# The last row frequency's transform back, moved into the next group's products

## The chip, the cores and the metric

The kernel runs on one core of a Trainium2 chip. The metric is device time in microseconds (us) of one execution; the time of a kernel is the median of its runs. Beside the times there is one profiled execution, with a record of every instruction on every engine (TensorE, VectorE, ScalarE, GpSimd, SyncE), of the DMA packets and of the clock that TensorE was granted.

## The reference

The program computes two layers on x of shape (16, 16, 256, 256). The change touches only the first, a Laplace neural operator with poles and residues, in this part of it:

```python
x = x + _L0_conv_ref(_gn(x), ...)          # layer 0
...
alpha = jnp.fft.fft2(x, axes=(-2, -1))
A  = 1.0 / (omega1[:, None, None, None] - weights_pole1[None])
Bm = 1.0 / (omega2[:, None, None, None] - weights_pole2[None])
S = jnp.einsum('ikpq,oikp,xikq->oxik', weights_residue, A, Bm)
output_residue1 = jnp.einsum('biox,oxik->bkox', alpha, S)
...
x1 = jnp.fft.ifft2(output_residue1, s=(Ny, Nx), axes=(-2, -1)).real
```

For every row frequency o and column frequency x a 16 by 16 matrix S mixes the channels of the spectrum; then the result is transformed back. The mix and the transform back along the columns (x) are the stage of the change; the transform along the rows is the next stage. Everything is in float32.

## The kernel before

The program is a string of stages. `layer0_forward` makes the spectrum of the normalised input and writes it to HBM as `al`; `layer0_mix` reads `al`, mixes the channels, transforms back along x and writes `hd`; `layer0_back` reads `hd`, transforms back along y, adds the input and normalises for layer 1; `layer1` is the rest. The change is in `layer0_mix`, which runs from about 1480 to 3050 us.

**Groups.** Real input makes the spectrum symmetric, so 128 row frequencies and one half are enough. `layer0_mix` goes over NF = 33 groups of four row frequencies; the last group has one (`range(4 if more else 1)`). For each group there are six kinds of work.

- `poles` (L609): six VectorE products spread a group's table of poles `av` to `lt`, the weights for the residues. There is one buffer for `lt` and two for `av`; `load_poles` (L599) loads the table of the group after next on SyncE's queue.
- `residues` (L623): TensorE makes S for the next group, two k at a time (eight calls, k0 = 0 to 14); each fills two PSUM tiles of the pool `psg`, copied to `s` by ScalarE for even k (L633) and VectorE for odd k (L631). There is one buffer for `s`.
- `expand` (L593, L595): the spectrum of four images (q of four) is spread to the block form `alb`, which all 16 images share; each q takes four operations, one or two on ScalarE and the others on VectorE. When it is done, `load_spectrum` (L582) loads the next one on SyncE's queue.
- `mix` (L642): the products proper. For each of 256 column frequencies i, a 128x32 weight tile `s[:, i]` is multiplied with `alb[:, i]` (128x64). Four at a time go to the four quadrants of 32 output partitions. There are eight blocks (`x0` = 0, 8, ..., 56) of 32 products each; each block fills one of four `psg` tiles and ScalarE copies it to `y` (L649). A float32 product is two matmul instructions, each with its weight load, so a mix is 512 matmuls and 512 loads, 64 of each in a block.
- `turn` (L658): for one row frequency f, eight TensorE transposes bring `y` into the layout for the transform; VectorE (L664) and ScalarE (L662) copy four of them each to `yt` (two buffers).
- `columns` (L675): the transform back of one row frequency f along x. 16 products (32 matmuls, 32 loads), eight for the even columns (`e` = 0) and eight for the odd ones (`e` = 1), go to two PSUM tiles `ph` (pool `psh`, two buffers). Then, for each tile, ScalarE copies the odd half (L684), VectorE makes sum and difference (L687, L688), and GpSimd issues the write to `hd` (L692), 256 KB.

**The order.** The whole stage is under `tc.manual_schedule` for TensorE, ScalarE, VectorE and GpSimd: each engine runs its instructions in the order of the program text, and only SyncE's loads are placed otherwise. For group g the order is: `mix` of g; `poles` and `residues` k0 = 0 for g + 1; then for each f: `turn`, two more calls of `residues` (one at f = 0), `expand` of q = f for g + 1, the next loads, `columns` of f. So `columns` of f = 3 stands between the last `residues` and `expand` for g + 1 and the `mix` of g + 1. Every product of a mix reads all 16 images of `alb`, and so needs all four expansions.

**Lines of the change.** `mix` gets a third argument; `columns` becomes a generator with a stop between `e` = 0 and `e` = 1; the loop over groups calls them in another order.

Of the kernel before, what the change touches and what calls it, by code (L numbers as in the profile page):

```python
# [547 lines left out]
def layer0_mix(ctx, tc, d, al, hd, tabs):  # L548
# [28 lines left out]
    def load_spectrum(g, q):  # L577

        t = gp.tile([P, 4, 2, P], F32, tag="alc", name="alc", bufs=4)
        src = al[g].rearrange("v (j h c) b x -> h (v j) c (b x)", h=2, c=8)  # L580
        for h in range(2):
            nc.sync.dma_start(  # L582
                out=t[64 * h : 64 * h + 64].rearrange("p b e x -> p (b e x)"),
                in_=src[h, :, :, 4 * q * N : 4 * q * N + 4 * N],
            )
        return t

    def expand(t, q):

        dst = alb.rearrange("p (x e) j b -> p b e x j", e=2)[:, 4 * q : 4 * q + 4]  # L590
        for j in range(4):
            if j <= q % 2:
                nc.scalar.activation(dst[..., j], t, AF.Copy, scale=m4[:, j : j + 1])  # L593
            else:
                nc.vector.tensor_scalar(dst[..., j], t, m4[:, j : j + 1], None, ALU.mult)  # L595

    def load_poles(g):
        av = ap.tile([P, 32, 4, 3], F32, tag="av", name="av")
        nc.sync.dma_start(out=av.rearrange("p k f l -> p (k f l)"), in_=avd[g])  # L599
        return av  # L600

    def poles(av):


        lt = lp.tile([P, 2, C, 3, 4, 8], F32, tag="lt", name="lt")
        shape = [P, C, 4, 8]
        for h in range(2):
            for plane in range(3):
                nc.vector.tensor_tensor(  # L609
                    lt[:, h, :, plane],  # L610
                    av[:, 16 * h : 16 * h + 16, :, plane].unsqueeze(3).to_broadcast(shape),
                    m8.unsqueeze(1).unsqueeze(2).to_broadcast(shape),
                    ALU.mult,
                )
        return lt

    def residues(lt, s, k0):

        for k in range(k0, k0 + 2):
            ps = psg.tile([P, 2, N], F32, tag="pg", name="ps")  # L620
            for v in range(2):
                for h in range(2):
                    nc.tensor.matmul(  # L623
                        ps[64 * h : 64 * h + 64, v],
                        lhsT=lt[:, h, k, 1 - v : 3 - v].rearrange("p l f c -> p (l f c)"),
                        rhs=tt[:, h, k],
                        start=True,
                        stop=True,
                    )
            if k % 2:  # L630
                nc.vector.tensor_copy(s[:, :, :, k], ps.rearrange("p v x -> p x v"))  # L631
            else:
                nc.scalar.copy(s[:, :, :, k], ps.rearrange("p v x -> p x v"))  # L633

    def mix(s, y):

        for x0 in range(0, 64, 8):
            ps = psg.tile([P, 8, 64], F32, tag="pg", name="pg")
            for x in range(8):
                for q in range(4):  # L640
                    i = 4 * (x0 + x) + q
                    nc.tensor.matmul(  # L642
                        ps[32 * q : 32 * q + 32, x],
                        lhsT=s[:, i].rearrange("p v k -> p (v k)"),
                        rhs=alb[:, i].rearrange("p j b -> p (j b)"),
                        start=True,
                        stop=True,
                    )
            nc.scalar.copy(y[:, :, x0 : x0 + 8], ps.rearrange("p x j -> p j x"))  # L649

    def turn(y, f):

        yt = hp.tile([P, 8, 8, C], F32, tag="yt", name="yt", bufs=2)
        for t0 in range(0, 8, 4):
            pt = pst.tile([P, 4, P], F32, tag="pt", name="pt")
            for t in range(4):
                j = 16 * f + 2 * (t0 + t)
                nc.tensor.transpose(pt[:, t], y[:, j : j + 2].rearrange("p q x -> p (q x)"), ident)  # L658
            dst = yt[:, :, t0 : t0 + 4].rearrange("p c t k -> p t c k")
            src = pt.rearrange("p t (c k) -> p t c k", k=C)  # L660
            if t0:
                nc.scalar.copy(dst, src)  # L662
            else:
                nc.vector.tensor_copy(dst, src)  # L664
        return yt

    def columns(g, f, yt):

        ph = [psh.tile([P, 2, N], F32, tag="ph", name="ph") for q in range(2)]
        for e in range(2):  # L670
            for n, (c, v) in enumerate(((0, 0), (0, 1), (1, 0), (1, 1))):
                i = 2 * (2 * c + e) + v
                for q in range(2):
                    lanes = slice(64 * q, 64 * q + 64)
                    nc.tensor.matmul(  # L675
                        ph[q][:, e],
                        lhsT=yt[lanes, i].rearrange("p t k -> p (t k)"),
                        rhs=ix[lanes, i],
                        start=n == 0,
                        stop=n == 3,  # L680
                    )
        for q in range(2):
            odd = hp.tile([P, 2, P], F32, tag="odd", name="odd", bufs=2)
            nc.scalar.copy(odd, ph[q][:, 1].rearrange("p (v x) -> p v x", v=2))  # L684
            o = hp.tile([P, 2, 2, P], F32, tag="h", name="h", bufs=5)
            even = ph[q][:, 0].rearrange("p (v x) -> p v x", v=2)
            nc.vector.tensor_tensor(o[:, :, 0], even, odd, ALU.add)  # L687
            nc.vector.tensor_tensor(o[:, :, 1], even, odd, ALU.subtract)  # L688
            o = o.rearrange("p v h x -> p v (h x)")
            fy = 4 * g + f  # L690
            if fy % P:
                nc.gpsimd.dma_start(  # L692
                    out=hd[fy, q:nb:2].rearrange("b k v x -> b (k v x)"),
                    in_=o.rearrange("p v x -> p (v x)"),
                )
            else:
                part = fy // P
                nc.gpsimd.dma_start(out=hd[0, q:nb:2, :, part], in_=o[:, 0])

    E = mybir.EngineType  # L700
    with tc.manual_schedule(engines={E.PE, E.Activation, E.DVE, E.Pool}):
        spectrum = [load_spectrum(0, q) for q in range(4)]
        lt = poles(load_poles(0))
        av = load_poles(1)
        s = gp.tile([P, N, 2, C], F32, tag="s", name="s")
        for k0 in range(0, C, 2):
            residues(lt, s, k0)
        for q in range(4):
            expand(spectrum[q], q)
            spectrum[q] = load_spectrum(1, q)  # L710
        for g in range(NF):
            more = g + 1 < NF
            y = gp.tile([P, 64, 64], F32, tag="y", name="y")
            mix(s, y)
            if more:
                lt = poles(av)
                s = gp.tile([P, N, 2, C], F32, tag="s", name="s")
                residues(lt, s, 0)
            for f in range(4 if more else 1):
                yt = turn(y, f)  # L720
                if more:
                    for k0 in range(2 if f == 0 else 4 * f, 4 * f + 4, 2):
                        residues(lt, s, k0)
                    expand(spectrum[f], f)
                    if g + 2 < NF:
                        if f == 0:
                            av = load_poles(g + 2)
                        spectrum[f] = load_spectrum(g + 2, f)
                columns(g, f, yt)


def exponential(nc, pool, y):
# [629 lines left out]
@with_exitstack  # L1362
def forward(ctx, tc, d):
    nb = d["x"].shape[0]
    dram = ctx.enter_context(tc.tile_pool(name="dram", bufs=1, space=DRAM))
    keep = ctx.enter_context(tc.tile_pool(name="keep", bufs=1))
    al = dram.tile([NF, 2, 64, nb, N], F32, name="al")
    bd = dram.tile([nb, P, P], F32, name="bd")
    hd = dram.tile([P, nb, C, 2, N], F32, name="hd")
    tabs = (  # L1370
        dram.tile([P, 2, C, N], F32, name="td"),
        dram.tile([NF, P, 384], F32, name="avd"),
        dram.tile([P, 2, C, N], F32, name="ed"),
    )
    zn = dram.tile([nb, C, N + 2, N + 2], F32, name="zn")
    cf = dram.tile([4, N + 2, 4, C, N], F32, name="cf")
    mr = keep.tile([P, nb, G, 2], F32, name="mr")
    layer0_forward(tc, d, al, bd, tabs)
    layer0_mix(tc, d, al, hd, tabs)
    layer0_back(tc, d, hd, bd, zn, mr, tabs[2])  # L1380
    layer1(tc, d, zn, cf, mr, nb)
# [25 lines left out]
```

## Time and profile before

| | us |
|---|---|
| time, median of 3 runs (7692.57 to 7713.86) | 7697.9 |
| the profiled execution's own time | 7702.15 |
| its span, first to last instruction | 7700.4 |
| TensorE busy with matmuls, of the span | 7126.0 |
| stretch 1480 to 3045 us (the mix stage): TensorE busy | 1379.6 of 1565 |
| same stretch: VectorE busy | 1007.9 |
| same stretch: ScalarE busy | 920.9 |
| same stretch: GpSimd busy | 153.2 |

The mean granted clock of TensorE was 0.965 over the span and 0.96 in the stretch of the mix. One group takes some 48 us of this stretch: about 14.7 us of mix and 33.6 us of all the rest.

How to read the lines that follow. A group line has the source line, the engine, the operation, the tiles (written <- read), the shape and the count; then busy time in all and the mean in ns of one; then the idle time of the engine just before these instructions and what ended most of it. "issue" is idle time in which the engine waited for no semaphore that the profile shows. A line of the timeline has the start and the busy time in us, then the same names, and in brackets the idle time before. PE is TensorE's matmuls, PEld its weight loads, DVE is VectorE, ACT ScalarE, POOL GpSimd, SP SyncE. Matmuls overlap, so that the mean of one is longer than the step from one to the next.

### The profile page before, as it was taken

To read this page: it belongs to the slowest core of one execution; us is meant where nothing else is said; L and a number is where in the kernel's file an instruction comes from. 1 tells how busy PE (TensorE), PEld (TensorE's weight loads), DVE (VectorE), ACT (ScalarE), POOL (GpSimd) and SP (SyncE) were. 2 spreads that over 40 slices of the span, in tenths; PEclk is the share of its full clock that TensorE was granted. 3 is DMA by queue.
4 is the path that set the end of the run, shared out by engine and by line. 5 is a ranking of instruction groups with operands and counts; after the bars stand their busy time and mean duration, and the time that the engine had idled before them with its cause. 6 is when DMAs were issued, how large, how long until landed. Compare 5 with 4: busy or idle time off the path is not lost. (4 is left out here: it accounts for less than half of the span.)

```text
span 7700.4 us, 147483 instructions
## 1 busy us (share of the span) xinstructions
PE 7126.0 (93%) x58728; PEld 4107.7 (53%) x58728; DVE 4921.2 (64%) x9184; ACT 3678.6 (48%) x5387; POOL 2804.5 (36%) x3616
## 2 busy tenths in 40 slices
PE   7889999688888988999978999999999999999997
PEld 5778888566666766777733333333333333333332
DVE  8999865366666665666656666666666666666662
ACT  2223333355555554111146656666566655656662
POOL 2334444200000000111135545555554555555552
PEclk9999999899999999999989999999999999999998
DMA  3444444333333333877757788898888898888896
GB/s 99 112 116 121 120 115 108 111 94 94 94 94 94 92 90 121 261 246 245 246 153 216 217 245 248 260 263 251 249 241 251 249 263 256 248 243 251 246 267 205
DMA packets 936290, 1442.20 MB, mean 187 GB/s; under 512 B 91866, under 2 KB 807958, under 8 KB 903606
## 3 DMA queue, kind: packets, MB, share of 16 engines
q1 hardware_dynamic: 792374, 958.51, 44.6%
q0 software_dynamic: 143232, 474.25, 19.4%
q8 instruction: 469, 7.68, 0.4%
q14 instruction: 215, 1.76, 0.1%
HBM read 875.87 MB, written 556.47 MB: 186 GB/s over the span
## 5 line engine op out<-in xcount | busy, mean ns | idle before, releaser
L995 ACT ACTIVATE wide<-c,b 32x512 f32<-32x512 f32 x2176 | 1479.5, 680 | 372.0 <-PE c L946 319.7
L1023 DVE TENSOR_TENSOR t<-pd,r 64x512 f32<-64x512 f32 x1088 | 744.4, 684 | 1321.8 <-PE pd L1015 1298.9
L1026 DVE TENSOR_TENSOR top<-pd,t 32x512 f32<-32x512 f32 x2176 | 1504.3, 691 | 54.8 <-DMA cf<-top 2.3
L1089 PE MATMUL c2ps<-rows,c 128*32 128x512 f32 x12288 | 1393.4, 600 | 20.6 <-ACT e L1098 14.7
L946 PE MATMUL c<-z,w 102*128 102x512 f32 x2048 | 1053.6, 646 | 140.1 <-ACT wide L995 116.3
L1007 POOL COPY wide<-wide 32x1031 f32<-32x1031 f32 (+1 forms) x576 | 570.1, 990 | 1390.1 <-ACT wide L995 1362.7
L1015 PE MATMUL pd<-wide,dw 128*128 128x512 f32 x2048 | 1012.7, 617 | 6.0 <-ACT r L983 3.2
L1089 PEld LDWEIGHTS c2ps<-rows,c 128*32 128x32 f32 x12288 | 388.7, 109 | 992.3 <-issue 885.1
L946 PEld LDWEIGHTS c<-z,w 102*128 102x128 f32 x2048 | 399.2, 197 | 703.8 <-issue 515.3
L1015 PEld LDWEIGHTS pd<-wide,dw 128*128 128x128 f32 x2048 | 376.7, 194 | 626.5 <-issue 458.2
L692 POOL DMA_DIRECT2D hd<-h x254 | 151.9, 598 | 1373.2 <-DVE h L688 1353.2
L631 DVE COPY s<-ps 128x512 f32<-128x512 f32 x264 | 271.4, 1028 | 508.5 <-PE ps L623 487.2
L1008 POOL COPY wide<-wide 32x1031 f32<-32x1031 f32 (+1 forms) x576 | 573.4, 996 | 35.9
L1098 ACT ACTIVATE e<-c2ps,b 128x512 f32<-128x512 f32 x256 | 176.0, 687 | 855.3 <-PE c2ps L1089 852.7
L313 PE MATMUL px<-wxn,u 128*64 128x256 f32 x4224 | 558.7, 385 | 2.1 <-ACT o L320 1.8
L813 PE MATMUL py<-h,iy 128*128 128x256 f32 x2048 | 541.5, 383 | 5.2 <-issue 5.2
L623 PE MATMUL ps<-tt,lt 128*64 128x256 f32 x4224 | 496.1, 385 | 37.9 <-DVE lt L609 37.3
L642 PE MATMUL pg<-alb,s 128*32 128x64 f32 x16896 | 310.6, 240 | 196.3 <-issue 185.2
L675 PE MATMUL ph<-ix,yt 64*128 64x256 f32 x4128 | 480.4, 382 | 0.7 <-ACT yt L662 0.7
L313 PEld LDWEIGHTS px<-wxn,u 128*64 128x64 f32 x4224 | 401.1, 136 | 127.4 <-ACT o L320 5.3
L813 PEld LDWEIGHTS py<-h,iy 128*128 128x128 f32 x2048 | 385.2, 191 | 108.4 <-issue 50.0
L675 PEld LDWEIGHTS ph<-ix,yt 64*128 64x128 f32 x4128 | 389.0, 187 | 89.9 <-issue 49.2
(202 smaller groups left out, 10343.7 us busy)
## 6 DMA issues: line engine op xcount, KB each, us to landing
rows<-cf SPq DMA_DIRECT2D x128, 2176.0 KB
z<-zn SPq DMA_DIRECT2D x768, 256.0 KB
cf<-top POOLq DMA_DIRECT2D x512, 240.0 KB, 7.3
cf<-bot POOLq DMA_DIRECT2D x96, 840.0 KB, 10.4
alc<-al SPq DMA_DIRECT2D x264, 256.0 KB
zn<-zb SPq DMA_DIRECT2D x128, 516.0 KB
o<-zn SPq DMA_DIRECT2D x64, 1032.0 KB
z<-in_x SPq DMA_DIRECT2D x64, 1024.0 KB
```

The source lines that it names most:

```text
L313: nc.tensor.matmul(ps[64 * k : 64 * k + 64, :, h], lhsT=u[:, h, part, g0 + j + k].rearrange("p f c -> p (f c)"), rhs=wxn[:, h, part], star ...
L623: nc.tensor.matmul(ps[64 * h : 64 * h + 64, v], lhsT=lt[:, h, k, 1 - v : 3 - v].rearrange("p l f c -> p (l f c)"), rhs=tt[:, h, k], start= ...
L675: nc.tensor.matmul(ph[q][:, e], lhsT=yt[lanes, i].rearrange("p t k -> p (t k)"), rhs=ix[lanes, i], start=n == 0, stop=n == 3,)
L813: nc.tensor.matmul(py[:, yh], lhsT=iy[:, v, ys], rhs=h[:, k, v], start=v == 0, stop=False)
L946: nc.tensor.matmul(ps[:, q], lhsT=w, rhs=cols[:, 1 - q], start=True, stop=True)
L995: nc.scalar.activation(self.feat[64 - 32 * q : 96 - 32 * q, f, self.groups[g], :H], ps[32 * f : 32 * f + 32, q], AF.Mish, bias=b1[0][32 * ...
L1007: nc.gpsimd.tensor_copy(flat[0:32, f, 1:m], flat[64:96, f, 0 : m - 1])
L1008: nc.gpsimd.tensor_copy(flat[96:128, f, 0 : m - 1], flat[32:64, f, 1:m])
L1015: nc.tensor.matmul(ps, lhsT=dwt if self.tail else dw, rhs=self.feat[:, f, cs, :H], start=True, stop=True,)
L1023: nc.vector.tensor_tensor(t[64:128], ps[:64], self.r[:, cs], ALU.mult)
L1026: nc.vector.tensor_tensor(self.top[32 * f : 32 * f + 32, cs, q], ps[lanes], t[lanes], ALU.add)
L1089: nc.tensor.matmul(ps[32 * j : 32 * j + 32], lhsT=c2[:, blk, dx, :], rhs=t[:, 4 * j + blk : 4 * j + blk + 4, x : x + H], start=(blk, dx) = ...
```

## The change

The transform back of the last row frequency of a group (f = 3) is no longer run at the end of the group. The generator `columns(g, 3, yt)` is made there, but nothing of it is issued until the next group's mix, which runs its first half (`e` = 0, 16 matmuls) ahead of block `x0` = 24 and the rest (`e` = 1, the odd copies, the sums and the two writes) ahead of block `x0` = 48. For f = 0, 1, 2, and for the one frequency of the last group, the generator is run out at once, so that the order there is as before. This happens in 32 of the 33 mixes; the first has an empty generator. Besides, `poles` of the next group is issued ahead of the mix and not behind it.

```diff
-    def mix(s, y):
+    def mix(s, y, between):
         for x0 in range(0, 64, 8):
+            if x0 in (24, 48):
+                next(between, None)
             ps = psg.tile([P, 8, 64], F32, tag="pg", name="pg")
...
         ph = [psh.tile([P, 2, N], F32, tag="ph", name="ph") for q in range(2)]
         for e in range(2):
+            if e:
+                yield
             for n, (c, v) in enumerate(((0, 0), (0, 1), (1, 0), (1, 1))):
...
+        between = iter(())
         for g in range(NF):
             more = g + 1 < NF
             y = gp.tile([P, 64, 64], F32, tag="y", name="y")
-            mix(s, y)
             if more:
                 lt = poles(av)
+            mix(s, y, between)
+            if more:
                 s = gp.tile([P, N, 2, C], F32, tag="s", name="s")
                 residues(lt, s, 0)
             for f in range(4 if more else 1):
...
-                columns(g, f, yt)
+                between = columns(g, f, yt)
+                if f < 3:
+                    for _ in between:
+                        pass
```

No instruction is added or taken away; only the order changes.

## The prediction

> **What bounds the kernel now.** I read the page first (busy rows, costliest groups), then the stretch 1480 to 3045 us in which the mix runs (its waits and DMA), then the timeline of one turn from group to group, and last the clock in slices of 3.4 us around single waits. The chain that ended last lies in later stages, but the whole program is a string of stages that wait for each other, so a microsecond that the mix gives up or takes is one of the total. In the mix TensorE is the bound, and the only large idle time is in the products on the quadrants:
>
> ```profile
> L642 PE MATMUL pg<-alb,s 128*32 128x64 f32 x16896 | 310.6, 240 | 196.3 <-issue 185.2
> L675 PE MATMUL ph<-ix,yt 64*128 64x256 f32 x4128 | 480.4, 382 | 0.7 <-ACT yt L662 0.7
> ```
>
> Line 642 stood idle for 196 us, almost all of it for "issue", that is for no semaphore at all. The matmuls of the transform back (line 675) wait for nothing. The waits of the stretch name what stands ahead of line 642's first matmul in each group:
>
> ```profile
> PE pg L642 <- issue: 172.4, 90, 4.8
> PE pg L642 <- ACT alb L593: 9.4, 32, 0.3
> ```
>
> 32 times, 0.3 us each, the mix waits for ScalarE to finish the expansion of the spectrum. The timeline of one turn shows why it is so little, and what the issue waits look like:
>
> ```profile
> 2003.67 1.90 PE L623 MATMUL ps<-tt,lt 128*64 128x256 f32 x16
> ...
> 2005.49 3.72 PE L675 MATMUL ph<-ix,yt 64*128 64x256 f32 x32
> 2005.57 3.89 ACT L593 ACTIVATE alb<-alc,m 128x1024 f32<-128x1024 f32 x2
> ...
> 2006.49 2.57 DVE L595 TENSOR_SCALAR alb<-alc,m 128x1024 f32<-128x1024 f32 x2
> ...
> 2009.51 3.44 PE L642 MATMUL pg<-alb,s 128*32 128x64 f32 x232 [0.29 <-ACT alb L593]
> ...
> 2010.76 1.26 POOL L692 DMA_DIRECT2D hd<-h  x2 [6.66 <-DVE h L688]
> 2011.04 3.69 DVE L609 TENSOR_TENSOR lt<-av,m 128x512 f32<-128x512 f32 x6
> ...
> 2015.41 1.99 PE L642 MATMUL pg<-alb,s 128*32 128x64 f32 x128 [2.46 <-issue]
> ...
> 2019.16 1.99 PE L642 MATMUL pg<-alb,s 128*32 128x64 f32 x128 [1.75 <-issue]
> ...
> 2022.90 0.54 PE L642 MATMUL pg<-alb,s 128*32 128x64 f32 x24 [1.75 <-issue]
> ```
>
> Two things are to be seen. First, the 3.72 us of line 675 (the last row frequency, f = 3) lie exactly beside the 3.89 us of line 593: they cover the expansion. Second, the mix restarts every 128 matmuls, 3.75 and 3.74 us apart (2015.41, 2019.16, 2022.90). 128 matmuls with 128 weight loads are 256 instructions, and the stretch has a DMA queue for just that (packets, MB, share of the engines); the second row is the writes of hd (count, KB each, us to landing):
>
> ```profile
> q8 instruction: 204, 3.34, 0.9%
> ...
> hd<-h POOLq DMA_DIRECT2D x254, 256.0 KB, 6.2
> ```
>
> 3.34 MB in 204 packets are 16.4 KB each; the mix is limited by the arrival of its own program, one page of 256 instructions per 3.74 us, against 1.9 us of work in it. Over the 32 mixes that the change touches (groups 1 to 32) single starts in the trace give: mix 14.7 us long on average, first page step 4.1 us, second 4.6, third 3.7.
>
> **The change, part by part.** Per group, 32 groups.
>
> (1) The transform of f = 3 leaves its place ahead of the mix. That frees 3.66 us of TensorE, but the mix can't start sooner: every product reads all 16 images of alb, and ScalarE's order ahead of the last expansion is untouched. TensorE now stands idle from the last residue matmul to 2009.51, by the starts in the trace 3.95 us where it was 0.29. Gain 0. The cover for the expansion is gone.
>
> (2) The same 64 instructions (32 matmuls, 32 loads) now stand in the mix, half of them after 3 of the 8 blocks, half after 6. If the pages set the pace, what they add is their share of a page: 64/256 x 3.74 = +0.94 us, and the other 2.7 us of work lie in time that was idle. Bounds: +0.44 (32 more pairs at 13.7 ns when no more page falls into the mix) and +3.66 (nothing hidden). I take 0.94: a half is 1.86 us, and with 112 pairs at 13.7 ns beside it a page holds 3.4 us of work, still under 3.74.
>
> (3) The writes of f = 3 to hd (two of 256 KB, 6.2 us to land) move from the front of the mix to its end. Now they land some 4 to 7 us into the mix, where the second page is asked for; that step takes 4.6 us where the third takes 3.7. Without them -0.85 us. Bounds: 0 (the spectrum loads of SP, which stay, are what holds the page up) and -1.2 (the first step falls to 3.74 as well). At the new place, after the sixth block and the VectorE sums, they meet code of 58 ns per instruction, where a page has 15 us to come.
>
> (4) The clock. After one long issue wait (2207.83 to 2212.33) it is halved, after one of 2.46 us it isn't:
>
> ```profile
> 2208.50:2212.00 3.50, 0.00 (x0) 0.00 (x0) 1.22 (x3) 0.00 (x0) 0.00 (x0) 0.99 0.77 237
> 2212.00:2215.40 3.40, 3.07 (x116) 3.07 (x120) 0.00 (x0) 0.62 (x2) 0.00 (x0) 0.50 0.03 11
> ...
> 2010.90:2014.30 3.40, 2.06 (x148) 1.89 (x136) 3.40 (x7) 1.54 (x3) 1.05 (x2) 1.00 0.65 171
> 2014.30:2017.70 3.40, 1.99 (x128) 1.83 (x128) 0.43 (x1) 1.17 (x2) 0.00 (x0) 1.00 0.63 204
> ```
>
> The columns: the stretch, its length, busy time (instructions) of TensorE's matmuls and loads, VectorE, ScalarE and GpSimd, then clock, DMA share and GB/s. 116 pairs at half clock take 3.07 us, 26.5 ns each against 13.7. In this trace every 3.4 us slice of the stage that had under 1.25 us of full-rate work was followed by one at 0.50. The new wait of 3.95 us always leaves such a slice, so nearly every mix now starts at half rate. Hidden is what falls behind a page; not hidden is the part ahead of the first page boundary, on average 64 pairs: 64 x (26.5 - 13.7) = 0.8 us, less what of the halved slice is spent in the wait itself. I take +0.7; bounds 0 and +1.7 (half of a slice).
>
> The Trainium skill ("TensorE: Matmul & The Clock Gate", Part 1) states that an idle window of about 3.4 us throttles the array to half, and that the window runs freely; the slices above agree. By the page alone the term would be up to 1.7 us, the sum +60 us. The skill's "Runtime: NRT & Kernel Launch", section "Instruction fetch mechanics", states that crossing a page of instructions is mostly hidden; by it the mix would have no idle time to fill and the change would cost (1)'s whole cover, +117 us. The restarts above contradict it.
>
> (5) TensorE changes its tile shape three times more per group. First columns matmul after the last residue: 0.31 us start to start, where pairs of the same kind follow in 0.22; so 0.1 each. Mostly behind the pages: +0.1, bounds 0 and +0.45.
>
> (6) At nothing: the poles (six of 684 ns on VectorE) run some 2 us earlier; their reader starts at the mix's end, 8.6 us after the old finish, so they had cover and keep it. SP's pole load waits for them and goes out 2 us earlier, 192 KB into a time with little traffic. Behind it SP has only the next group's spectrum. The two odd copies (377 ns) now stand ahead of the last two y copies on ScalarE; the transposes start 1.2 us after the last y copy today, and ScalarE idles for most of the mix. If that cover failed, 0.65 us. The four sums (0.41 us) are done before the first residue copy needs VectorE. POOL idles up to 24.6 us for its two issues. PSUM ph, yt and h are wanted again only after the next group's first transposes.
>
> Sum: 0 + 0.94 - 0.85 + 0.7 + 0.1 = +0.89 us per group, x 32 = **+28 us**. The profiled execution took 7702.15 us (span 7700.4), 4 us over the median; I add the sum to the median 7697.9: **7726 us**. A measurement of this kernel tells about 0.3%, 23 us, from no change.
>
> **The rivals.**
>
> A. As summed, chance 0.52, own range 7685 to 7755: the terms' signs differ, and 0.15 us per group decides whether it passes 0.3%.
>
> B. The halves aren't hidden (0.22). Place: the half-rate clock holds through the first half, which then takes 3.7 us instead of 1.86, and the page behind it has come long before; and the page steps shrink by half of what I take when the writes move. Price: (2) rises by 1.86 to 2.8, (3) is -0.4, (4) and (5) stay: 3.2 us, x 32 = +102, 7800 us, from 7770 to 7815. For it: halved slices followed by another halved one when the mix in them was thin. Against it: a slice full of mix at half rate (124 matmuls) was always followed by a full clock.
>
> C. Faster (0.23). One mechanism: pages come sooner. The first is asked for during the new wait, so that what lies ahead of its boundary (64 pairs, 0.88 us at full rate, and with it (4)) is no longer on the path, and without the writes each step is 3.74 (-1.2). With the lower bound of (2): 0.44 - 1.2 = -0.76 us, and up to -0.88 more; half of that gives -1.2, x 32 = -38 us, 7660, from 7646 to 7674. It decides from where page steps average under 3.75 and the first boundary costs nothing. For it: third steps at 3.47 to 4.02. Against: spectrum loads still run for the first 5 us, and mixes whose boundary came at once still waited 3.4 us.
>
> D. It doesn't do what it says, the mix starts at once when the transform is gone (0.03): -3.66 x 32 + 28 = -89, 7609 us. Against it stands the row of 32 waits for alb.
>
> **How the numbers follow.** The point is A's. A lies over the 0.3% line with 0.29, inside with 0.23; B is slower, 0.22; C is faster with 0.17, inside with 0.06; D 0.03 faster. Slower 0.51, same 0.29, faster 0.20. The range runs from 7660, C's centre, to 7805, past B's: outside it D, half of C and a third of B, 0.2 in all.
>
> **What would show it.** Right: line 642's first matmul waits some 3.9 us for alb in 32 groups (about 125 us), its issue idle falls from 185 us to under 110, the clock is 0.50 at the start of nearly every mix, mixes with the halves inside last 15.6 us on average, and second page steps fall under 4 us. Wrong: no wait for alb; issue idle unchanged; or halves that take 1.9 us each with page waits as long as before.

## The result and the profile after

The changed kernel took 7702.5 us (median of 4 runs, 7698.7 to 7711.1) beside 7698.3 us of the kernel before: ratio 1.0004, interval 0.9987 to 1.0021. In a longer series (11 runs beside 15 of the kernel before, label e11_again) the ratio was 1.0011, interval 1.0002 to 1.0021, which is +8 us, between +2 and +16. So the change made the kernel about 0.1% slower: 8 us where 28 were forecast, on the side that was forecast, inside the 0.3% that the prediction called no change.

The groups of the page after the change, with the same columns as before (line 642 is now 645, line 675 now 680):

```profile
L680 PE MATMUL ph<-ix,yt 64*128 64x256 f32 x4128 | 493.6, 386 | 3.5 <-issue 2.6
L645 PE MATMUL pg<-alb,s 128*32 128x64 f32 x16896 | 320.0, 242 | 177.9 <-ACT alb L593 124.2
```

and the waits of the mix stage (1480 to 3050 us): us in all, times, longest

```profile
PE pg L645 <- ACT alb L593: 124.2, 32, 3.9
...
PE pg L645 <- issue: 53.4, 39, 12.9
```

The idle time ahead of the products went from 196 to 178 us only, but it changed its kind. In the waits, 172.4 us for instructions became 53.4. One wait of 12.9 us in the 53.4 stands ahead of the first mix, outside the change; the 172.4 are without it, because the first mix of the kernel before began at 1479.6, just ahead of the window. So like compared with like, 172.4 us became 40.5. And 9.4 us for the expansion became 124.2, 32 waits of 3.9 us. One turn in the timeline:

```profile
2008.19 3.67 PE L623 MATMUL ps<-tt,lt 128*64 128x256 f32 x32
...
2011.87 3.83 ACT L593 ACTIVATE alb<-alc,m 128x1024 f32<-128x1024 f32 x2
...
2015.75 4.54 PE L645 MATMUL pg<-alb,s 128*32 128x64 f32 x192 [3.89 <-ACT alb L593]
2020.22 2.00 PE L680 MATMUL ph<-ix,yt 64*128 64x256 f32 x16
2022.14 1.09 PE L645 MATMUL pg<-alb,s 128*32 128x64 f32 x61
2023.42 1.99 PE L645 MATMUL pg<-alb,s 128*32 128x64 f32 x128 [0.19 <-issue]
2026.89 0.30 PE L645 MATMUL pg<-alb,s 128*32 128x64 f32 x3 [1.48 <-issue]
2027.13 2.00 PE L680 MATMUL ph<-ix,yt 64*128 64x256 f32 x16
2029.05 2.39 PE L645 MATMUL pg<-alb,s 128*32 128x64 f32 x128
```

To be seen: TensorE does nothing while ScalarE expands (2011.87 to 2015.70); the first 192 matmuls then take 4.54 us where at full clock they take 2.89 (shown under e5); the two halves stand where page waits of 2.46 and 1.75 us stood in the turn shown of the kernel before. The clock in slices around this wait (stretch, length, busy time of PE, PEld, DVE, ACT, POOL, then clock, DMA share, GB/s):

```profile
2012.70:2016.10 3.40, 0.35 (x24) 0.35 (x28) 3.40 (x5) 3.00 (x2) 0.00 (x0) 1.00 0.50 175
2016.10:2019.50 3.40, 3.40 (x146) 3.40 (x138) 2.69 (x5) 0.95 (x2) 0.00 (x0) 0.51 0.37 117
2019.50:2022.90 3.40, 3.40 (x119) 2.84 (x114) 0.00 (x0) 0.81 (x2) 0.00 (x0) 0.99 0.46 105
```

By the clock's records 30 of the 32 mixes start at half rate or fall to it within their first 2 us.

The following table is made from single records of each trace: the 32 mixes of groups 1 to 32, first to last product with all that stands between; the start of the first packet of the instruction queue after the mix's start; the steps from packet to packet; the clock at the mix's start, and how much of a mix lay at half clock. A mean over 32 mixes of one execution is good to about 0.2 us, since single mixes lie 1 us apart.

| kernel | mix, us | first packet | step 1 | step 2 | clock at start | half clock, us of a mix | one group to the next |
|---|---|---|---|---|---|---|---|
| before | 14.72 | 2.40 | 4.74 | 3.61 | full | 3.48 | 48.38 |
| after | 14.75 | 2.62 | 3.99 | 3.71 | half | 3.43 | 48.47 |
| after, again (e11) | 14.82 | 2.58 | 3.86 | 3.83 | half | 3.44 | 48.52 |
| e1 writes moved alone | 13.77 | 2.27 | 3.96 | 3.71 | full | 1.48 | 47.58 |
| e2 f = 3 left out | 13.83 | 2.66 | 3.79 | 3.69 | half | 4.19 | 47.51 |
| e6 e2, clock kept | 13.76 | 2.48 | 3.85 | 3.70 | full | 1.91 | 47.54 |
| e3 after, longer spin | 14.10 | 2.34 | 3.80 | 3.81 | full | 0.53 | 50.86 |
| e5 after, clock kept | 15.17 | 2.66 | 3.86 | 3.91 | full | 0.75 | 48.91 |
| e9 f = 3 whole | 15.60 | 2.63 | 4.17 | 4.27 | half | 3.94 | 49.35 |
| e4 one step later | 15.49 | 2.37 | 4.68 | 3.60 | full | 0.75 | 45.58 |
| e8 e4, writes late | 14.98 | 2.36 | 3.99 | 3.73 | full | 0.96 | 45.02 |
| e10 e8, load late | 13.95 | 1.77 | 3.73 | 3.73 | full | 0.43 | 44.22 |

Two things in these records bear on the whole account. First, the restarts are waits for instructions: in the trace before, all 84 waits of over 0.4 us within these mixes end at the same place of a page, when TensorE's instructions are counted in order by 256, and each ends 1.2 to 1.6 us after a packet of the instruction queue has ended. Second, the half clock is not new. In the kernel before, 25 of the 32 mixes already had a stretch at half clock, from 5 us after their start on (the slice 2212.00:2215.40 in the prediction is one of them), 3.48 us of a mix on average. The change moved this stretch to the front of the mix; the total, 3.43 us, stayed.

### The profile page after: what moved, and what is told of

Its sections match the earlier page's. It is cut to its first block, busy times and chain, and to the rows that moved or that the text cites. A ratio compares the mean times of both kernels' runs of the same rounds, so it can differ in the third digit from the quotient of the medians.

```text
span 7703.9 us, 147451 instructions
## 1 busy us (share of the span) xinstructions
PE 7142.5 (93%) x58728; PEld 4117.4 (53%) x58728; DVE 4910.9 (64%) x9184; ACT 3678.2 (48%) x5387; POOL 2797.1 (36%) x3616
## 5 line engine op out<-in xcount | busy, mean ns | idle before, releaser
L1099 PE MATMUL c2ps<-rows,c 128*32 128x512 f32 x12288 | 1391.9, 599 | 20.0 <-ACT e L1108 13.7
L645 PE MATMUL pg<-alb,s 128*32 128x64 f32 x16896 | 320.0, 242 | 177.9 <-ACT alb L593 124.2
L207 PE MATMUL pu<-fy,eo 128*128 128x128 f32 x2048 | 426.6, 292 | 9.5 <-DVE u L224 5.6
```

What stands on the lines that cost most here:

```text
L1099: nc.tensor.matmul(ps[32 * j : 32 * j + 32], lhsT=c2[:, blk, dx, :], rhs=t[:, 4 * j + blk : 4 * j + blk + 4, x : x + H], start=(blk, dx) = ...
```

## The experiments

**e1: the writes alone.** The matmuls stay ahead of the mix; copies, sums and writes come later. The poles stay early, as in the changed kernel, so their part isn't separated here.

```diff
-            if x0 in (24, 48):
+            if x0 == 48:
                 next(between, None)
...
-            if e:
-                yield
...
+        yield
         for q in range(2):
             odd = hp.tile([P, 2, P], F32, tag="odd", name="odd", bufs=2)
...
                 between = columns(g, f, yt)
+                next(between)
```

> All matmuls of f = 3 stay ahead of the mix as before; only its odd copies, sums and the two writes to hd are issued ahead of block x0 = 48, and the poles ahead of the mix. Theory (the writes hold up the second page of instructions, and cover, clock and matmuls are as before): the mix falls from 14.72 us to about 13.9, the second page step from 4.74 us to about 4.0, clock at the start of the mix 1.00, 32 x -0.8 = -25 us, 7673 us. Rival (SP's spectrum loads hold the page up, which stay): mix 14.7 us, 7698 us.

Measured: 7676.6 us beside 7708.7, ratio 0.9959 (0.9944 to 0.9974); mix 13.77 us, first step 3.96. The theory holds, and the part of the change that gains is worth 0.4% alone. With fewer long page waits, the half clock fell too, from 3.48 to 1.48 us of a mix.

**e2: what is left when f = 3 is left out.**

```diff
+                if f == 2:
+                    nc.gpsimd.dma_start(
+                        out=hd[fy + 1, q:nb:2].rearrange("b k v x -> b (k v x)"),
...
-                between = columns(g, f, yt)
-                if f < 3:
-                    for _ in between:
+                if f < 3:
+                    for _ in columns(g, f, yt):
                         pass
```

> The changed kernel without the transform back of f = 3 in groups 0 to 31 (its matmuls, copies and sums are left out; the row is written with the tile of f = 2, beside f = 2's own writes). What is left is the wait for alb, the halved clock, and a mix without writes in it. Theory (wait takes the whole place of the transform; halved clock costs the mix some 0.2 us): wait for alb 3.9 us in 32 groups, mix 14.1 us, so the whole is only about 20 us under the kernel before although 117 us of TensorE work are gone: 7675 to 7685 us. If the halved clock costs 0.7 us as I predicted: mix 14.6 us, 7695. Rival (the transform had been on the path and not beside the expansion): the mix starts 3.7 us sooner, 7580 us.

Measured: 7681.7 us in one run. The wait is that of the changed kernel:

```profile
PE pg L645 <- ACT alb L593: 124.2, 32, 3.9
```

117 us of TensorE work are gone and the time falls by 27 us (7708.7 to 7681.7), no more than the 32 us that e1 gained by the writes: the transform had cost nothing where it stood. The mix, with no writes and no halves but started at half clock (4.19 us of a mix), took 13.83 us, as short as that of e1, started at full clock (1.48 us). This spoke against the clock term of the prediction. It also gives the halves' own price: 14.75 - 13.83 = 0.92 us.

**e3, e5, e6: the clock kept at the start.** Products that nobody reads fill the wait; 16 of them in e3, 8 in e5, and 8 on top of e2 in e6.

```diff
                 lt = poles(av)
+            if g:
+                spin()
             mix(s, y, between)
...
+    def spin():
+        pt = pst.tile([P, 4, P], F32, tag="pt", name="spin")
+        for n in range(8):
+            nc.tensor.matmul(
+                pt[:, 2 * (n % 2) : 2 * (n % 2) + 2].rearrange("p a b -> p (a b)"),
+                lhsT=ident, rhs=ix[:, n % 8], start=True, stop=True,
+            )
```

> The changed kernel with 16 products of 128 x 256 that nobody reads (32 matmuls, 32 loads, about 3.5 us) ahead of each mix, in the wait for alb; so that the clock isn't halved. Theory with the predicted clock term: mix with the halves falls from 14.75 us to 14.05, 32 x -0.7 = -22 us, 7680 us. Theory with a clock term of 0.2 us: mix 14.55, -6 us, 7696 us. Rival (the halved clock costs nothing, all behind the pages): no change, 7702 us, and the 64 added instructions cost nothing either.

Measured: 7789.6 us, ratio 1.0106 (1.0091 to 1.0121). The expectation had the products' price wrong: with 128 rows each they took 7.17 us for 16, where the transform's, with 64 rows, take 3.7. The mix began 3.2 us late in every group, and so this run tells nothing by its time. Its mixes took 14.10 us, 0.65 less than the changed kernel's, just what the predicted clock term asks for. But with the mix 3.2 us later a good part of the spectrum load lay ahead of it, and this run can't tell the two apart; e5 takes the clock alone, e10 the load alone.

> The changed kernel with 8 products that nobody reads in the wait for alb (in e3 16 of them took 7.2 us, 3.2 us more than the wait; 8 should take 3.6). The mix starts where it did, the clock is 1.00. If the halved clock costs what I predicted, 0.7 us per group: mix 14.75 -> 14.05, 32 x -0.7 = -22 us against the changed kernel. If it costs what e2 beside e1 shows (13.83 against 13.77 us): mix 14.7, no change. The 64 instructions alone must cost nothing, since they pass at 112 ns each.

Measured: 7716.2 us (10 runs) beside 7708.4, ratio 1.0012 (1.0003 to 1.0022); the changed kernel in e11 had 1.0011. (8 products are 32 instructions, not 64 as the expectation says.) One turn of its timeline:

```profile
2014.49 3.72 PE L709 MATMUL spin<-ix,ident 128*128 128x256 f32 x16
2018.52 2.89 PE L645 MATMUL pg<-alb,s 128*32 128x64 f32 x192 [0.31 <-ACT alb L593]
2021.34 2.00 PE L680 MATMUL ph<-ix,yt 64*128 64x256 f32 x16
2023.27 0.42 PE L645 MATMUL pg<-alb,s 128*32 128x64 f32 x13
2024.15 1.99 PE L645 MATMUL pg<-alb,s 128*32 128x64 f32 x128 [0.47 <-issue]
2028.17 0.97 PE L645 MATMUL pg<-alb,s 128*32 128x64 f32 x51 [2.03 <-issue]
```

The first 192 matmuls take 2.89 us again, 1.65 less than at half clock, and the page waits behind them grow from 1.67 (0.19 + 1.48) to 2.50 us (0.47 + 2.03). In this one turn that leaves a gain. Over all mixes it doesn't: the waits for instructions grow from 40.5 to 83.7 us (without the 12.9 ahead of the first mix), 1.35 us per mix, and the mix takes 15.17 us against 14.75, of which some 0.3 belong to this execution, 10 us over its kernel's median. By the times of e5 and e11, each good to 0.1%, the clock can still cost up to some 0.3 us per group; the 0.7 us are refuted.

> e2 (f = 3 left out) with the same 8 products in the wait. Without the halves in the mix, theory (at half clock a page of 128 pairs still takes 3.4 us, less than it waits for the next page): mix 13.8 us as in e2. If the clock costs 0.7 us there too: 13.1.

Measured: 7673.4 us in one run, mix 13.76 us beside e2's 13.83, with 1.91 us of a mix at half clock beside 4.19. Of the 8 us between the two times 7 lie ahead of the mix stage, which began that much sooner in e6. Without the halves the clock's price is 0.07 us, between means that are good to 0.2; it is not 0.7.

**e7: is it pages, or the array?**

```diff
-            for x in range(8):
+            for x in range(0, 8, 2):
...
-                        ps[32 * q : 32 * q + 32, x],
+                        ps[32 * q : 32 * q + 32, x : x + 2].rearrange("p x j -> p (x j)"),
                         lhsT=s[:, i].rearrange("p v k -> p (v k)"),
-                        rhs=alb[:, i].rearrange("p j b -> p (j b)"),
+                        rhs=alb[:, i : i + 2].rearrange("p i j b -> p (i j b)"),
```

> The kernel before with 128 products per mix where it had 256, each over the alb of two frequencies (128 columns), so that the array streams the same columns with half the instructions; half of the products take the neighbour's weights, so the result is not the reference's. Theory (the mix waits for pages of instructions): two pages less, 2 x 3.74 = 7.5 us less, mix 7.2 us, 33 x -7.5 = -247 us, 7455 us. Rival (the quadrants or the array set the pace): mix 14.7 us, 7700 us.

Measured: 7474.5 us in one run beside 7708.4, -234 us. A turn of its timeline, the mix and the first products behind it:

```profile
2021.84 7.20 PE L642 MATMUL pg<-alb,s 128*32 128x128 f32 x256 [0.29 <-ACT alb L593]
2028.96 1.95 PE L623 MATMUL ps<-tt,lt 128*64 128x256 f32 x16
```

256 matmuls run through without a wait, 28 ns each for 128 columns; in the kernel before a matmul of 64 columns takes 13.7 ns where no page is awaited, so the columns stream as fast. So the array needs 7.2 us for a mix, and what made it 14.7 is the arrival of instructions. The mean over 32 mixes is 7.66 us, since some still wait for a page (8 waits, 10 us in all), and the fall of 234 us is 13 short of the theory.

**e9: the transform in one piece.** e1 with `x0 in (24, 48)` and without the early `next(between)`.

> The changed kernel with all 32 matmuls of f = 3 ahead of block x0 = 24 and its copies, sums and writes ahead of x0 = 48 as they were. Theory (a page of instructions hides work up to 3.7 us less its own): the page that holds the whole transform has some 5 us of work, 1.2 us too much, so the mix grows from 14.75 us to 15.4 to 16.0, 32 x +0.6 to +1.2 = +20 to +40 us on the changed kernel. Rival (only the sum of work and pages counts, not where it stands): no change.

Measured: 7736.7 us, ratio 1.0044 (1.0031 to 1.0058), mix 15.60 us. Against e11's 1.0011 that is 25 us, 0.8 us per group. A page can hide one half but not the whole.

**e4, e8, e10: the cover given back.** In e4 every transform waits until the turn and residues of the next row frequency have been issued. So f = 2 stands beside the last expansion, and f = 3 in the mix.

```diff
-                between = columns(g, f, yt)
-                if f < 3:
-                    for _ in between:
-                        pass
+                for _ in between:
+                    pass
+                between = columns(g, f, yt)
+                if not more:
+                    for _ in between:
+                        pass
```

> The changed kernel with the transform back of each f behind the turn and residues of f + 1, so that f = 2 stands beside the last expansion and f = 3 in the next mix. Theory (the change lost the cover of 3.66 us, and nothing else of it is bad): the wait for alb falls back to 0.3 us, the clock at the start of the mix stays 1.00, the group's period falls from 48.47 us to 44.1 to 44.8 us, 7702 - 32 x (3.7 to 4.4) = 7561 to 7584 us. Rival (VectorE and ScalarE, which now get the copies of f beside the expansion of f + 1, set the pace in the row frequencies): TensorE waits for yt or s there, and the time is 7640 us or more.

Measured: 7625.4 us, ratio 0.9894 (0.9877 to 0.9910): better than both kernels, but 41 to 64 us short of the theory. The wait for alb is gone (9.4 us in 32 times) and the clock is full, as expected, and TensorE waits for no copy. What was missed stands in the table: now the writes of f = 2 land in the mix, the first step is 4.68 us as in the kernel before, and the mix 15.49. e8 moves these writes:

```diff
+            if x0 == 48:
+                while late:
+                    fy, q, o = late.pop(0)
+                    nc.scalar.dma_start(
...
-            if fy % P:
+            if f == 2:
+                late.append((fy, q, o))
+            elif fy % P:
```

> e4 (f = 2 beside the expansion, f = 3 in the mix) with the two writes of f = 2 issued by ScalarE ahead of block x0 = 48 in place of GpSimd at once. In e4 these writes land where those of f = 3 did, and the second page step was 4.68 us. Theory: the step falls to 3.7 to 4.0 us, the mix from 15.49 to 14.6 us or less, the period from 45.58 to 44.7, 7625 - 32 x 0.9 = 7596 us. Rival (it is the spectrum loads, or the sums on VectorE, that hold the mix of e4 up): no change.

Measured: 7597.8 us, ratio 0.9859 (0.9844 to 0.9874); first step 3.99. The time is as forecast within 2 us, but with some luck: the mix fell only to 14.98 us where 14.6 or less was forecast, and the period to 45.02 where 44.7 was. The last one, e10, moves SP's spectrum load of q = 3 to the same place:

```diff
-                        spectrum[f] = load_spectrum(g + 2, f)
+                        if f < 3:
+                            spectrum[f] = load_spectrum(g + 2, f)
...
+                if 0 < g < NF - 1:
+                    spectrum[3] = load_spectrum(g + 1, 3, nc.scalar)
```

> e8 with the spectrum load of q = 3 issued by ScalarE ahead of block x0 = 48 in place of SP at the start of the mix, so that nothing but pages and the poles' table is moved in the first two thirds of the mix. Theory (what is left above 3.6 us in the first page steps is the spectrum load; in e3, where it ran 3.2 us earlier, the mix was 0.6 us shorter than in the changed kernel): first step 3.99 to 3.7 us, mix 14.98 to 14.4 us, 32 x -0.5 = -16 us, 7582 us. Rival (the load at 8 of 16 engines doesn't delay a page): no change, 7598 us.

Measured: 7571.9 us, ratio 0.9831 (0.9817 to 0.9844). The first packet comes after 1.77 us in place of 2.36, the first step is 3.73, the mix 13.95 us. With the same writes and nearly the same clock, the load delays pages as the writes do. Its waits:

```profile
PE pg L656 <- issue: 66.5, 45, 12.9
...
PE pg L656 <- ACT alb L593: 9.4, 32, 0.3
```

This version beats both kernels, the one before by 1.7%. It has a price of its own, which the timeline shows: ScalarE spends 0.6 us on each issue, and its last two copies of y come late.

```profile
2026.28 1.26 ACTq L648 DMA_DIRECT2D hd<-h  x2
2027.57 1.07 ACT L663 COPY y<-pg 128x512 f32<-128x512 f32 x2 [2.40 <-DMA hd<-h]
```

**e11: the changed kernel again.**

> The changed kernel again, for a narrower interval and a second profile beside these. Theory: within 0.2% of the kernel before; mix 14.6 to 14.9 us.

Measured: as told with the result, 7712.3 us beside 7704.4; mix 14.82 us.

## Why the prediction was right, and where it wasn't

Case A came, at a third of its size. Halves and writes nearly cancel, as forecast; that the point lay 20 us too high is mostly the work of one term, the clock's. The range held the result easily, so the test lies in the steps. Per group:

| step | forecast | measured | from |
|---|---|---|---|
| (1) start of the mix | no gain, wait 3.95 | no gain, wait 3.88 (124.2 / 32) | waits after |
| (2) halves by pages, with (5) | +0.94 + 0.1 | +0.92 | after less e2 |
| (3) writes out of the mix | -0.85 | -0.95 | e1 less before |
| (4) halved clock | +0.7 | +0.07 | e2 less e6 |
| sum | +0.89 | +0.04 | the rows; 14.75 less 14.72 is 0.03 |

The rows are steps of one chain, before, e1, e6, e2, after (e1 and e6 differ by 0.01), so that their sum must agree; the test lies in the single rows, each good to some 0.3 us.

(1) was right, and e2 shows it from the other side: the transform's 3.7 us had been free. The 2.8 us that the mix hides of them were paid for with a wait of 3.9, and only the move of the writes, which the change brings by the way, kept the balance even.

(2) was right, and came closer than the means are good for, which is luck. Its bound was right too: a half fits into a page, the whole doesn't (e9). In the trace after, the 6 mixes whose first page boundary lies within their first 28 pairs, so that one more boundary falls into them, last 15.8 us, the other 26 last 14.5; in e11 it is 15.9 and 14.6. At full clock the halves' price, e5 less e6, is 1.41 us, or 1.1 without what belongs to that execution. Its ground, that the mix waits for instructions, is shown by e7.

(3) was right, though e1 doesn't separate the writes from the poles' earlier load; the bound of 0, that the spectrum load alone holds the page up, is refuted by e1. But the load has a share too, which the sum left out: without it the mix falls from 14.98 us (e8) to 13.95 (e10).

(4) is the step that failed. That nearly every mix would start at half clock was right (30 of 32). Two things were wrong. The term counted the half clock as new, but the mixes of the kernel before had as much of it, only later (3.48 us of a mix, 3.43 after). And the price was wrong: "not hidden is the part ahead of the first page boundary", 0.8 us. Where the clock alone was given back, nothing was gained (e5: 0.75 us of a mix at half clock, mix 15.17; e6 beside e2: 1.91 and 4.19, mixes 13.76 and 13.83). The first page is not asked for later at half rate: its packet starts 2.62 and 2.58 us into the mix, and 2.66 us in e5 at full rate. That the sequencer reads on ahead of slow matmuls would explain it, but this was only argued; no run separates it. What the runs show is the exchange: 1.65 us more for the first matmuls in one turn, and 1.35 us per mix less of page waits. The bound of 0 was the right end, and e2 beside e1 could have been foreseen from the row of 3.07 us for 116 pairs: a page at half rate takes 3.4 us, still under the step of 3.74. Without this term the sum is +0.19, or +6 us, where +8 was measured. For the same reason one of the signs that the prediction named for being right did not come: the mixes last 14.75 us, not 15.6.

(6), the work put at nothing, holds as far as waits show it: apart from alb the waits after name no new wait of TensorE above 3 us in all.

Rival B (+102 us) fell with the page waits, 172 to 40.5 us, and with the first half, which took 2.1 us on average and not 3.7. Rival C (-38 us) needed a first packet that comes sooner; it came no sooner (2.62 us against 2.40). D fell with the row of 32 waits. The mix accounts for +1 to +3 us of the measured +8 (0.03 to 0.10 us x 32), the whole group for 3 to 5 (0.10 to 0.14 us x 32); the rest is within what executions differ by and wasn't traced.

## What to carry to other kernels

Before work is moved into an engine's idle time, ask what it covered where it stood: here the same 3.7 us were free beside an expansion, and moving the neighbour into that place (e4) turned a zero into 1%. Where an engine waits for nothing that the profile names, look at the rate of its instructions and at the queue that brings them: 256 instructions per 3.7 us was the limit here. Two things paid: to fill its waits with work whose old place had another use (e4, 83 us), and to move other transfers out of its way (e1 32 us, e8 28, e10 26). And before a halved clock is charged to a change, see how much of it was there already, and whether the engine at half rate still outruns its feed: here a page took 3.4 us at half clock against 3.7 for the next to come, and the clock's price was too small to measure.

## What the runs showed of the hardware

Data transfers hold up the arrival of instructions: the step between two pages was 4.74 us while writes of 512 KB landed (before), 3.96 without them (e1) and 3.73 without the spectrum load too (e10); and without that load the first packet of instructions started 0.6 us sooner (e10 against e8). 16 products over 128 rows took 7.17 us (e3), 16 of the transform over 64 rows, which follow each other on the two halves of the rows, 3.7 us. And a DMA issue by ScalarE held that engine for 0.6 us (e10).
